# Attention with image prompts on one core: the last batch's turns, scores and query chunk in other places, and the root of the batch before it behind the last exponentials

## The chip, the core and the metric

The kernel runs on one NeuronCore of a Trainium2 chip. The metric is the time of one execution on the device, in microseconds (us). The core's engines each work through their own instructions in order and wait for one another through semaphores: PE (TensorE, matmuls; PEld is its weight load), DVE (VectorE), ACT (ScalarE), POOL (GpSimdE), and SP (SyncE), which here issues nearly all DMA transfers.

## The reference

`x` has 8 batches of 112 queries by 320 channels, the context 8 batches of 375 rows by 512 (371 of text, 4 of image prompts); there are 20 heads of 16 channels.

```python
def _l2norm(x, axis=-1):
    n = jnp.sqrt(jnp.sum(x * x, axis=axis, keepdims=True))
    return x / jnp.maximum(n, EPS)
...
text_ehs = encoder_hidden_states[:, :-NUM_TOKENS]
ip_ehs = encoder_hidden_states[:, -NUM_TOKENS:]
...
q = heads(hidden_states @ W_q)
k_t = heads(text_ehs @ W_k)
v_t = heads(text_ehs @ W_v)
scores_t = jnp.einsum('bhsd,bhtd->bhst', q, k_t) * attn_scale
probs_t = jax.nn.softmax(scores_t, axis=-1)
text_out = jnp.einsum('bhst,bhtd->bhsd', probs_t, v_t)
...
k_ip = heads(ip_ehs @ W_k_ip)
v_ip = heads(ip_ehs @ W_v_ip)
attn_scores = jnp.einsum('bhsd,bhnd->bhsn', q, k_ip) * attn_scale
qsem = jnp.einsum('bhst,bte->bhse', probs_t, text_ehs)
qsem = _l2norm(qsem)
ip_n = _l2norm(ip_ehs)
sem = jnp.einsum('bhse,bne->bhsn', qsem, ip_n)
...
fused = attn_scores + SEM_SCALE * sem
probs_ip = jax.nn.softmax(fused, axis=-1)
probs_ip = probs_ip * spatial_mask[None, None, :, None]
ip_out = jnp.einsum('bhsn,bhnd->bhsd', probs_ip, v_ip)
...
out = text_out + IP_SCALE * ip_out
out = out @ W_out + b_out
out = out + residual
```

## The kernel before

Batches are numbered 0 to 7; "the sixth batch" is number 6, "the last" number 7. The 20 heads of a batch form five groups of four. All numbers are 32-bit floats.

**A group's way.** `scores` multiplies a head's queries (`qm`, scaled and masked by `project_queries`) by its keys `kT` into one PSUM bank. `maxima` reduces it on DVE (`nmx`), `exponentials` takes the exponential on ACT into `p` and copies four prompt columns into `ipl`. `sent` has SP move the exponentials into one of two buffers `xg`, laid out in 32-row blocks, and `turned` transposes such a buffer on DVE into `xgT`, in pieces; a piece is one `next`. `multiplied` is the main work of PE: twelve steps `j`, in each of which four heads multiply `xgT` by a piece of `u`, with 392 columns at the first step and 32 fewer at each further one. `u` holds the context's Gram matrix (`gram`), since the norm in the reference is a quadratic form of the probabilities, and behind it the values, which `placed` copies for the next group on POOL in three copies, one per four steps. Each of them overwrites what four steps of the group before read, and each is waited for by the four steps that read it.

**The sums behind a group.** The quadratic form of a head is the row sum of a product of the bank and `p`. `reduced` does both on DVE in one pass (`junk`). To spare DVE, `shared` does some heads otherwise, in three pieces: copies on ACT into `shared` (and of the 21 columns that hold the prompts' products, the sum of exponentials and the values into `pvs`), products on POOL, row sums on ACT into `ss`. The last group of batch 6 has two heads done so, groups 0 to 3 of batch 7 have 3, 3, 2 and 1.

**A batch's end.** `finish` is cut into pieces too: `z2` and the reciprocal `zr` on DVE and `attn` on POOL; `rn` on DVE, its root on ACT, with ACT's table of functions loaded for the root ahead of it and for the exponential behind it; the logits `fu` on DVE; their exponential `ex`; the weights `w`; and then matmuls, which for batch 6 come after all groups of batch 7.

**Order.** It is written by hand: each engine takes its instructions in the order in which the code emits them. The main loop goes over batches 0 to 6 and within each group emits the scores and the turns of groups to come; batch 7 has a loop of its own at the end, which the change rewrites. There group g's banks come from `ps_qd` (four banks) for even g and from the two small pools of two banks for odd g. The scores of group 3 use the small pools' banks, which group 1 takes next; those of group 4 use `ps_qd`'s, which group 0 had and group 2 takes next. The last chunk of channels of batch 7's queries (`ps_q_7_2`, heads of group 4) are projected between groups 0 and 1.

## Time and profile before

| | |
|---|---|
| median of 3 runs (lowest to highest) | 410.84 us (410.69 to 410.94) |
| the profiled execution: its time, and its span from first to last instruction | 410.67 us, 409.0 us |
| mean granted clock of PE | 0.989 |
| ACT, DVE, POOL, share of the span busy | 47%, 83%, 29% |
| transfers, share of 16 DMA engines | about 52%; next to none in the last 20 us |
| last batch's loop, first matmul of group 0 to the first step behind group 4 | 364.88 to 397.16 us of the span |
| last write of the output issued | 405.98 us of the span |

The page gives each engine's busy time and cuts the span into 40 slices with a digit for the busy tenths, and a line PEclk for the share of PE's clock that was granted. The chain of waits is read backward from the last instruction: at each step what released it. The order of time lists an engine's instructions with their start, length and, in brackets, how long the engine stood idle ahead of them and who ended that. Windows give the busy time of each engine in a stretch.

### The profile page before, as it was taken

How to read it: one execution, taken by the hardware profiler on the slowest of the kernel's cores; microseconds unless marked ns; L12 is line 12 of the kernel's file. 1: busy time of each engine (PE TensorE's matmuls, PEld its weight loads, DVE VectorE, ACT ScalarE, POOL GpSimd, SP SyncE). 2: the span in 40 equal slices, each digit the busy share in tenths (PEclk: the TensorE clock that was granted, in tenths of full speed). 3: DMA queues.
4: the chain of work that ended last, by engine and by line, in shares of the span. 5: the costliest groups of instructions: out<-in, count | busy, mean ns of one | idle time of the engine just before them, and what ended most of it. 6: DMA issues, size and time to landing. Idle time of an engine off the chain costs nothing.

```text
span 409.0 us, 13891 instructions
## 1 busy us (share of the span) xinstructions
PE 400.4 (98%) x5442; PEld 314.2 (77%) x5442; DVE 340.3 (83%) x731; ACT 191.7 (47%) x663; POOL 118.3 (29%) x282
## 2 busy tenths in 40 slices
PE   9999999999999999999999999999999999996996
PEld 8658777987788877787778877788777977785893
DVE  4678787888998898788998989788998888877774
ACT  3554243454344633446344543456334463567663
POOL 6611110111432206122162214222060211735340
PEclk9999999999999999999999999999999999997999
DMA  6984665556555556366555555465444455444200
GB/s 215 216 184 112 218 170 150 143 159 175 144 138 136 153 137 153 105 169 168 133 143 126 151 138 139 120 148 158 128 119 120 122 172 142 119 119 125 67 3 30
DMA packets 46433, 56.94 MB, mean 139 GB/s; under 512 B 9405, under 2 KB 40961, under 8 KB 46368
## 3 DMA queue, kind: packets, MB, share of 16 engines
q1 hardware_dynamic: 46328, 55.99, 51.9%
q8 instruction: 43, 0.70, 0.7%
q14 instruction: 22, 0.18, 0.1%
q10 hardware_dynamic: 40, 0.07, 0.0%
HBM read 15.88 MB, written 1.39 MB: 42 GB/s over the span
## 4 chain that ended last, share of the span: by engine, by line
PE 96%; ACT 1%; issue 1%; POOL 1%; DVE 1%; POOLq 0%; DVEq 0%
PE ps_qd L729 41%; PE ps_k L547 15%; PE ps_s L658 11%; PE ps_v L547 10%; PE ps_g L513 7%; PE ps_q L363 4%; PE ps_o L949 3%; PE ps_g L469 1%; PE ps_w L448 1%; PE ps_o L900 1%; POOL shared L764 0%; PE ps_a L937 0%; DVE xgT L710 0%; PE ps_c L432 0%; PE ps_ipkv L298 0%
## 5 line engine op out<-in xcount | busy, mean ns | idle before, releaser
L729 PE MATMUL ps_qd<-u,xgT 32*112 32x168 f32 (+11 forms) x3840 | 218.2, 352 | 0.0
L729 PEld LDWEIGHTS ps_qd<-u,xgT 32*112 32x112 f32 x3840 | 185.5, 173 | 26.3 <-issue 2.3
L694 ACT ACTIVATE p<-ps_s,nmx 112x371 f32<-112x371 f32 x156 | 84.5, 579 | 97.3 <-DVE nmx L680 92.3
L710 DVE STREAM_TRANSPOSE xgT<-xg 128x512 f32<-128x512 f32 (+2 forms) x79 | 125.9, 1602 | 1.1 <-DMA xr_sb<-in_x_dram 0.5
L680 DVE TENSOR_REDUCE nmx<-ps_s 112x1 f32<-112x371 f32 x160 | 78.7, 536 | 28.1 <-PE ps_s L658 23.6
L775 DVE CUSTOM_DVE_ANT_0 junk<-ps_qd,p 112x371 f32<-112x371 f32 x146 | 79.3, 543 | 20.1 <-ACT pvs L742 4.0
L627 POOL COPY u<-vr 128x64 f32<-128x64 f32 x120 | 26.5, 240 | 145.4 <-PE ps_qd L729 100.3
L658 PE MATMUL ps_s<-kT,qm 32*112 32x375 f32 (+1 forms) x320 | 65.4, 497 | 0.0
L547 PE MATMUL ps_k<-ctxT,wk_sb 128*128 128x371 f32 x192 | 64.6, 484 | 0.0
L547 PEld LDWEIGHTS ps_k<-ctxT,wk_sb 128*128 128x128 f32 x192 | 35.1, 190 | 20.3 <-ACT vT L569 0.5
L547 PE MATMUL ps_v<-ctxT,wv_sb 128*128 128x371 f32 x128 | 42.4, 482 | 0.0
L658 PEld LDWEIGHTS ps_s<-kT,qm 32*112 32x112 f32 x320 | 25.6, 173 | 12.8 <-issue 11.0
L547 PEld LDWEIGHTS ps_v<-ctxT,wv_sb 128*128 128x128 f32 x128 | 23.7, 190 | 14.5 <-issue 0.5
L513 PE MATMUL ps_g<-ctxT 128*32 128x375 f32 (+11 forms) x672 | 30.4, 333 | 0.0
L513 PEld LDWEIGHTS ps_g<-ctxT 128*32 128x32 f32 x672 | 27.7, 110 | 2.0
L562 ACT COPY kT<-ps_k 128x371 f32<-128x371 f32 x24 | 11.2, 468 | 37.8 <-PE ps_k L547 37.8
L696 ACT COPY ipl<-ps_s 112x4 f32<-112x4 f32 x140 | 23.1, 165 | 0.0
L420 DVE STREAM_TRANSPOSE ctxT<-ct 128x512 f32<-128x512 f32 x21 | 22.7, 1093 | 0.0
L924 POOL TENSOR_TENSOR wv<-vip,w 112x1280 f32<-112x1280 f32 x6 | 14.8, 2465 | 26.5 <-DVE w L858 26.5
L363 PE MATMUL ps_q<-xT,wq_sb 128*128 128x224 f32 (+1 forms) x90 | 17.5, 335 | 3.5 <-ACT shared L760 3.5
L485 ACT ACTIVATE ug<-ps_g 128x375 f32<-128x375 f32 (+2 forms) x24 | 8.3, 375 | 24.4 <-issue 9.0
L569 ACT COPY vT<-ps_v 128x371 f32<-128x371 f32 x16 | 7.5, 468 | 25.4 <-PE ps_v L547 25.4
(164 smaller groups left out, 313.2 us busy)
## 6 DMA issues: line engine op xcount, KB each, us to landing
xg<-p SPq DMA_DIRECT2D x156, 162.3 KB
u<-ug SPq DMA_DIRECT2D x122, 99.0 KB
ct<-in_ctx_dram SPq DMA_DIRECT2D x28, 176.0 KB
vip<-vipd SPq DMA_DIRECT2D x6, 560.0 KB
xr_sb<-in_x_dram SPq DMA_DIRECT2D x32, 35.0 KB
out_dram<-ob SPq DMA_DIRECT2D x8, 140.0 KB
x_sb<-in_x_dram SPq DMA_DIRECT2D x6, 140.0 KB
xg<-wv_sb SPq DMA_DIRECT2D x4, 162.3 KB
```

The lines of the kernel that those rows point to most:

```text
L363: nc.tensor.matmul(ps[:, : n * S], wq_sb[:, j, i * P : (i + 1) * P], xT[:, j, :n, :, : S // QN], start=(j == 0), stop=(j == NC - 1),)
L420: nc.vector.transpose(ctxT[:, :, c * P : (c + 1) * P].rearrange("p e (j i) -> p j e i", i=RG), ct[:, some, :].rearrange("p j (k e) -> p j ...
L513: nc.tensor.matmul(ps[c][q * RG : (q + 1) * RG, j * RG - c * P : T - c * P], ctxT[:, e, j * RG : (j + 1) * RG], ctxT[:, e, j * RG : T], st ...
L547: nc.tensor.matmul(ps[:, :TT], w[:, e, i * P : (i + 1) * P], ctxT[:, e, :TT], start=(e == 0), stop=(e == NE - 1),)
L627: nc.gpsimd.tensor_copy(v, dealt(b, c, s["vr"][:, c * QN : (c + 1) * QN, min(g + g // NE, 2 * NC - 1), :]))
L658: nc.tensor.matmul(ps[:S, :w], qm[a * RG : (a + 1) * RG, i, r, j * S : (j + 1) * S], s["kT"][a * RG : (a + 1) * RG, i, :w], start=True, st ...
L680: nc.vector.tensor_reduce(nmx, s["sc", g, a][:S, :TT], AX.X, ALU.max, negate=True)
L694: nc.scalar.activation(s["p", g][:, a, :], ps[:S, :TT], AF.Exp, bias=nmx)
L696: nc.scalar.copy(s["ipl"][:, groups[g][a], :], ps[:S, TT:T])
L710: nc.vector.transpose(xT[:, j0:j1].rearrange("p j (k q) -> p q j k", q=QN), xg[:, :, j0 * RG : j1 * RG].rearrange("p q (j k) -> p q j k", ...
L729: nc.tensor.matmul(banks[a][:S, j * RG : UW], xT[a * RG : (a + 1) * RG, j, :S], region(b, c)[a * RG : (a + 1) * RG, q, j * RG - c * P :], ...
L775: nc.vector.tensor_tensor_reduce(out=junk, in0=ps[:S, :TT], in1=s["p", g][:, a, :], scale=1.0, scalar=0.0, op0=ALU.mult, op1=ALU.add, accu ...
```

## The change

Only the last batch's loop is rewritten, and two special cases in `project_queries` go. The queries' last chunk is projected ahead of group 0, into the common banks, and scaled on ACT. `finish` of batch 6 begins behind group 0 instead of ahead of it; the second and third pieces of the row sums shared with ACT are emitted later; its root, with both table loads, stands behind the last exponentials. `turned` is taken in halves, with maxima between them. The scores of group 4 move from steps 2 and 3 of group 1 to steps 5 and 6. The later pieces of `finish` come one or two places later.

```diff
--- before.py
+++ after.py
@@ -339,7 +339,6 @@
 
     def project_queries(bs):
         n = len(bs)
-        end = bs[0] == B - 1
         xT = work.tile([P, NC, 2, QN, RG], F32, tag="xT", name=f"xT_{bs[0]}", bufs=1)
         qm = work.tile([P, NC, 2, 2 * S], F32, tag="qm", name=f"qm_{bs[0]}", bufs=2)
 
@@ -355,10 +354,7 @@
                 )
             yield
         for i in range(NC):
-            if end and i == FULL:
-                ps = ps_qd.tile([P, 512], F32, tag="qd", name=f"ps_q_{bs[0]}_{i}")
-            else:
-                ps = bank(f"ps_q_{bs[0]}_{i}", spare=(bs[0], i) == (1, 1))
+            ps = bank(f"ps_q_{bs[0]}_{i}", spare=(bs[0], i) == (1, 1))
             for j in range(NC):
                 nc.tensor.matmul(
                     ps[:, : n * S],
@@ -369,9 +365,7 @@
                 )
 
             for r in range(2 if i < FULL else 1):
-                by = nc.vector.tensor_scalar_mul
-                if qT is None and not (end and i == FULL):
-                    by = nc.scalar.mul
+                by = nc.scalar.mul if qT is None else nc.vector.tensor_scalar_mul
                 by(qm[:, i, r, : n * S], ps[:, : n * S], emask[:, r : r + 1])
             if qT is not None:
                 nc.scalar.copy(qT[:, i, :], ps[:, :S])
@@ -1291,42 +1285,38 @@
             drain(prompt_logits(b))
 
 
-    next(sums)
     b = B - 1
     before = ("f", b - 1)
-
-    run(before, lambda: finish(b - 1, bd=bd[:, 0]))
-    with_bias(b - 1)
-    nc.scalar.preload_act_table(AF.Sqrt)
+    next(sums)
+    run(("q", b), None)
 
     for g in range(NG):
-        if g == 1:
-            run(("q", b), None)
-            drain(sums)
         for j, _ in enumerate(multiplied(b, g)):
-            if g == 0 and j == 0:
-                drain(sums)
             if g == 0 and j in (0, 3):
-                for a in (2, 3) if j == 0 else (0, 1):
+                some = (2, 3) if j == 0 else (0, 1)
+                for a in some:
                     scores(b, NG - 2, a, ps=bank(f"ps_s_{b}_{NG - 2}_{a}", spare=a > 1))
+                for a in some:
+                    probabilities(b, NG - 2, a, hold=True)
                 if j == 0:
-                    for a in (2, 3):
-                        maxima(b, NG - 2, a)
-                    run(before, None)
-                    for a in (2, 3):
-                        exponentials(b, NG - 2, a)
-                    drain(turned(b, 1))
-                    for a in (2, 3):
+                    turn = turned(b, 1)
+                    next(turn)
+                else:
+                    drain(turn, sums)
+                    for a in (2, 3, 0, 1):
                         sent(b, NG - 2, a)
-                else:
-                    for a in (0, 1):
-                        probabilities(b, NG - 2, a)
-            if g == 1 and j in (2, 3):
-                for a in ((3, 2), (1, 0))[j - 2]:
+            if g == 1 and j in (5, 6):
+                for a in ((3, 2), (1, 0))[j - 5]:
                     ps = ps_qd.tile([P, 512], F32, tag="qd", name=f"ps_s_{b}_{NG - 1}_{a}")
                     scores(b, NG - 1, a, ps=ps)
-                    probabilities(b, NG - 1, a)
-            if (g, j) in ((1, QN), (1, 2 * QN), (2, 2 * QN)):
+                    probabilities(b, NG - 1, a, hold=True)
+                if j == 6:
+                    drain(turn)
+                    for a in (3, 2, 1, 0):
+                        sent(b, NG - 1, a)
+                    nc.scalar.preload_act_table(AF.Sqrt)
+                    run(before, None)
+            if (g, j) in ((2, QN), (2, 2 * QN), (3, QN)):
                 run(before, None)
             if g > 1 and j == 2 * QN:
                 drain(sums)
@@ -1335,15 +1325,21 @@
         if g == NG - 1:
             break
         n = (3, 3, 2, 1)[g]
-        sums = shared(b, g, n)
+        earlier, sums = sums, shared(b, g, n)
         next(sums)
         reduced(b, g, n)
         if g < NG - 2:
             value_sums(b, g, n)
-            drain(turned(b, g + 2))
+            turn = turned(b, g + 2)
+            if g == 0:
+                next(turn)
+            else:
+                drain(turn, earlier)
             placed(b, g + 1, range(NT) if g == 0 else (NT - 1,))
             next(sums)
         if g == 0:
+            run(before, lambda: finish(b - 1, bd=bd[:, 0]))
+            with_bias(b - 1)
             with_bias(b)
             run(("f", b - 2), None)
         if g == 2:
```

The lines of the changed program are four to six less than those of before, so `L710` and `L704` are one line of code.

**DVE, from the sums of batch 6's last group on.** Names: `junk` and `ss` are `reduced`, `z`, `zr`, `rn` are `finish` of batch 6, `nmx_3_2` is the maximum for group 3's head 2, `xgT_1` the turned group 1. Before:

```order
L825 SCALAR_TENSOR_TENSOR z_6_0_5235<-pvs_3352 112x20
L816 RECIPROCAL zr_0_5237<-pvs_3352 112x20
L680 TENSOR_REDUCE nmx_3_2_5258<-ps_s_3_2_5254 112x1
L680 TENSOR_REDUCE nmx_3_3_5260<-ps_s_3_3_5256 112x1
L830 TENSOR_TENSOR rn_0_5236<-ss_3351,z_6_0_5235 112x20
L710 STREAM_TRANSPOSE xgT_1_5269<-xg_151 128x4x192 x2
L680 TENSOR_REDUCE nmx_3_0_5290<-ps_s_3_0_5286 112x1
L680 TENSOR_REDUCE nmx_3_1_5295<-ps_s_3_1_5288 112x1
L775 ISA junk_6_5339,ss_4038<-ps_qd_0_3_5247,p_0_4977 112x371
L775 ISA ss_4038 112x1
L710 STREAM_TRANSPOSE xgT_2_5342<-xg_152 128x4x192 x2
L375 TENSOR_SCALAR qm_4305<-ps_q_2_5353,emask 128x112
```

and with the change:

```order
L674 TENSOR_REDUCE nmx_3_2_5252<-ps_s_3_2_5248 112x1
L674 TENSOR_REDUCE nmx_3_3_5256<-ps_s_3_3_5250 112x1
L704 STREAM_TRANSPOSE xgT_1_5260<-xg_151 128x4x192
L674 TENSOR_REDUCE nmx_3_0_5278<-ps_s_3_0_5274 112x1
L674 TENSOR_REDUCE nmx_3_1_5282<-ps_s_3_1_5276 112x1
L704 STREAM_TRANSPOSE xgT_1_5260<-xg_151 128x4x192
L769 ISA junk_6_5332,ss_4038<-ps_qd_0_3_5243,p_0_4977 112x371
L769 ISA ss_4038 112x1
L704 STREAM_TRANSPOSE xgT_2_5335<-xg_152 128x4x192
L819 SCALAR_TENSOR_TENSOR z_6_0_5343<-pvs_3352 112x20
L810 RECIPROCAL zr_0_5345<-pvs_3352 112x20
L674 TENSOR_REDUCE nmx_4_3_5384<-ps_s_4_3_5382 112x1
```

`z`, `zr` and `rn` no longer stand ahead of group 1's turn (`rn`, which waits for ACT's sums, comes five rows further on than the rows shown), the maxima of group 3's heads 0 and 1 stand between its halves, and the last maxima between the halves of group 2's turn.

**POOL, from batch 6's products on.** Names: `ob` and `xb` are outputs and residuals, `shared` the products, `attn` the divided values, `u<-vr` is `placed`. Before:

```order
L913 TENSOR_TENSOR ob_5230<-ob_5230,xb_4703 112x320
L764 TENSOR_TENSOR shared_4_5215<-shared_4_5215,p_4_4839 112x371 x2
L817 TENSOR_TENSOR attn_153<-pvs_3352,zr_0_5237 112x320
L789 TENSOR_TENSOR xb_5238<-x_sb,bias_sb 112x320
L627 COPY u_4035<-vr_4036 128x4x16 x3
L764 TENSOR_TENSOR shared_0_5332<-shared_0_5332,p_0_4977 112x371 x3
L789 TENSOR_TENSOR bd<-x_sb,bias_sb 112x320
L627 COPY u_4035<-vr_4036 128x4x16 x3
L764 TENSOR_TENSOR shared_1_5453<-shared_1_5453,p_1_5038 112x371 x3
```

and with the change:

```order
L907 TENSOR_TENSOR ob_5230<-ob_5230,xb_4703 112x320
L758 TENSOR_TENSOR shared_4_5215<-shared_4_5215,p_4_4839 112x371 x2
L621 COPY u_4035<-vr_4036 128x4x16 x3
L758 TENSOR_TENSOR shared_0_5325<-shared_0_5325,p_0_4977 112x371 x3
L811 TENSOR_TENSOR attn_153<-pvs_3352,zr_0_5345 112x320
L783 TENSOR_TENSOR xb_5346<-x_sb,bias_sb 112x320
L783 TENSOR_TENSOR bd<-x_sb,bias_sb 112x320
L621 COPY u_4035<-vr_4036 128x4x16 x3
L758 TENSOR_TENSOR shared_1_5441<-shared_1_5441,p_1_5038 112x371 x3
```

`attn` and `xb` moved from ahead of group 1's placing to behind the three products of group 0, and the placing of group 2's values still stands behind them.

**ACT, from group 0's row sums on.** Names: `p_4` are group 4's exponentials, `ex` and `rn` belong to `finish` of batch 6, `shared_1` is group 1's copy. Before:

```order
L768 ACTIVATE shared_0_5332,ss_4038<-shared_0_5332 112x371 x3
L694 ACTIVATE p_4_5381<-ps_s_4_3_5377,nmx_4_3_5379 112x371
L696 COPY ipl_4037<-ps_s_4_3_5377 112x4
L694 ACTIVATE p_4_5381<-ps_s_4_2_5385,nmx_4_2_5387 112x371
L696 COPY ipl_4037<-ps_s_4_2_5385 112x4
L694 ACTIVATE p_4_5381<-ps_s_4_1_5396,nmx_4_1_5398 112x371
L696 COPY ipl_4037<-ps_s_4_1_5396 112x4
L694 ACTIVATE p_4_5381<-ps_s_4_0_5403,nmx_4_0_5405 112x371
L696 COPY ipl_4037<-ps_s_4_0_5403 112x4
L850 ACTIVATE ex_0_5439<-fu_0_5416 112x80
L759 COPY pvs_4039<-ps_qd_1_0_5361 112x21
L760 COPY shared_1_5453<-ps_qd_1_0_5361 112x371
```

and with the change:

```order
L688 ACTIVATE p_4_5386<-ps_s_4_3_5382,nmx_4_3_5384 112x371
L690 COPY ipl_4037<-ps_s_4_3_5382 112x4
L688 ACTIVATE p_4_5386<-ps_s_4_2_5389,nmx_4_2_5391 112x371
L690 COPY ipl_4037<-ps_s_4_2_5389 112x4
L688 ACTIVATE p_4_5386<-ps_s_4_1_5399,nmx_4_1_5401 112x371
L690 COPY ipl_4037<-ps_s_4_1_5399 112x4
L688 ACTIVATE p_4_5386<-ps_s_4_0_5405,nmx_4_0_5407 112x371
L690 COPY ipl_4037<-ps_s_4_0_5405 112x4
L1317 ACT_TABLE_LOAD
L828 ACTIVATE rn_0_5344<-rn_0_5344 112x20
L829 ACT_TABLE_LOAD
L753 COPY pvs_4039<-ps_qd_1_0_5353 112x21
```

The sums of group 0 moved behind the copies of group 1, and between the last exponentials and those copies stand two table loads with the root between them. Before, the two loads and the root stood ahead of the exponentials of group 3.

## The prediction

> **What bounds the kernel now.** I read the page first (engines, slices), then the chain of waits over the last 90 us, then windows of the stretch that stands out, then each engine's order of time there.
>
> ```profile
> span 409.0 us, 13891 instructions
> PE 400.4 (98%) x5442; PEld 314.2 (77%) x5442; DVE 340.3 (83%) x731; ACT 191.7 (47%) x663; POOL 118.3 (29%) x282
> PE   9999999999999999999999999999999999996996
> PEclk9999999999999999999999999999999999997999
> ```
>
> PE sets the time: busy 98%, every slice full but one near the end, and in that slice the granted clock is low too. The chain of waits shows what happens there.
>
> ```profile
> 356.50 0.67 PE ps_q L363 x6
> ...
> 368.88 0.03 DVE rn L830
> ...
> 370.68 1.17 issue
> 371.84 0.49 DVE nmx L680
> ...
> 373.59 0.38 ACT shared L760
> ...
> 374.01 1.63 PE ps_q L363 x6
> 375.63 4.37 PE ps_qd L729 x26
> ```
>
> Group 0 of the last batch is finished, and PE waits. What it waits for runs from `rn` (the root's operand of the sixth batch) through both half-turns and the maxima on DVE, then exponentials and copies on ACT, to the queries' last chunk. The windows price it (columns: length, PE, PEld, DVE, ACT, POOL busy, granted clock, DMA share, GB/s).
>
> ```profile
> 364.96:370.51 5.55, 5.55 (x104) 5.14 (x104) 3.00 (x9) 4.32 (x8) 3.42 (x4) 1.00 0.63 174
> 370.51:374.01 3.50, 0.00 (x1) 0.00 (x1) 3.50 (x7) 2.90 (x13) 1.39 (x4) 0.86 0.11 24
> 374.01:375.63 1.62, 1.62 (x10) 1.42 (x10) 1.62 (x2) 1.50 (x7) 1.60 (x2) 0.50 0.63 184
> 375.63:380.00 4.37, 4.37 (x33) 2.56 (x36) 0.60 (x2) 1.24 (x5) 1.93 (x3) 0.51 0.32 97
> 392.51:397.16 4.65, 4.65 (x99) 4.60 (x93) 3.34 (x14) 3.21 (x10) 2.07 (x4) 1.00 0.01 4
> 372.00:373.00 1.00, 0.00 (x0) 0.00 (x0) 1.00 (x3) 0.64 (x3) 0.27 (x2) 1.00 0.00 0
> 373.00:374.00 1.00, 0.00 (x0) 0.00 (x0) 1.00 (x3) 1.00 (x6) 0.00 (x0) 0.52 0.38 83
> 379.00:380.00 1.00, 1.00 (x12) 0.61 (x12) 0.00 (x0) 0.00 (x0) 0.00 (x0) 0.56 0.00 0
> 380.00:381.00 1.00, 1.00 (x22) 0.90 (x20) 0.58 (x2) 0.00 (x0) 0.00 (x0) 1.00 0.00 0
> ```
>
> PE stands still for 3.50 us, and the clock falls to half at about 373.0, some 2.5 us after PE stopped, until about 379.9. The place thus costs three things: 3.50 of idling; 1.63 - 0.67 = 0.96 for the six `ps_q` instructions at half clock (the same six took 0.67 at 356.50); and half of the 4.25 us from 375.63 to 379.88, 2.12, for group 1. Sum **6.58**: what there is to win. Without it the five groups would end at 397.16 - 6.58 = 390.6. A group with four scores takes 5.55 (first row), one without 4.65 (fifth row).
>
> **The change part by part.** Where "after" times stand below, they are sums from the rows, on before's time axis; up to 363 the order is the same.
>
> *Queries' last chunk ahead of group 0.* The six instructions now follow L949 at full clock: 0.67, so group 0 ends at 371.18 instead of 370.51. Its bank is free, as its earlier user's exponentials lie far back. Its scaling moves from DVE to ACT, ahead of the exponentials, into the place of a table load. That is no extra term: the 0.67 is already in the 6.58.
>
> *Root off DVE's and ACT's front, turns in halves.*
>
> ```profile
> 366.47 1.00 DVE L680 TENSOR_REDUCE nmx<-ps_s 112x1 f32<-112x371 f32 x2 [1.13 <-PE ps_s L658]
> 368.88 0.18 DVE L830 TENSOR_TENSOR rn<-ss,z 112x20 f32<-112x20 f32 x1 [1.42 <-ACT shared L768]
> 369.06 2.93 DVE L710 STREAM_TRANSPOSE xgT<-xg 128x768 f32<-128x768 f32 x2
> 371.84 0.94 DVE L680 TENSOR_REDUCE nmx<-ps_s 112x1 f32<-112x371 f32 x2
> 372.36 0.57 ACT L694 ACTIVATE wv_sb<-ps_s,nmx 112x371 f32<-112x371 f32 x1 [0.58 <-DVE nmx L680]
> 372.87 0.58 ACT L694 ACTIVATE wv_sb<-ps_s,nmx 112x371 f32<-112x371 f32 x1
> 373.44 0.51 ACT L760 COPY shared<-ps_qd 112x371 f32<-112x371 f32 x1
> 373.87 0.53 ACT L760 COPY shared<-ps_qd 112x371 f32<-112x371 f32 x1
> ```
>
> DVE stood 1.42 us for the sixth batch's sums. Now: two maxima from 366.47 + 0.67 = 367.14, first half-turn 368.0 to 369.5 (2.93 for two), the other maxima to 370.4, second half-turn to 371.9. The exponentials follow at a pitch of 0.51 and are done, with their small copies, at 371.15. Group 1 takes the four banks of these scores; its first matmuls need the first half-turn (369.5) and the exponentials, its seventh step the second half-turn, over 3 us later. So it starts at about 371.2, with 0 to 0.2 us of waiting; I take **0.1**. The old gap is gone. The transposes' sources have landed: the row of 372 to 373 has a DMA share of 0.00, and the next are sent at 371.9 (SP's order is unchanged, first send 372.06 before).
>
> *What the moved work meets: POOL.*
>
> ```profile
> 366.32 1.90 POOL L764 TENSOR_TENSOR shared<-shared,p 112x371 f32<-112x371 f32 x2
> 368.18 0.74 POOL L817 TENSOR_TENSOR attn<-pvs,zr 112x320 f32<-112x320 f32 x1
> 370.88 0.86 POOL L789 TENSOR_TENSOR xb<-x_sb,bias_sb 112x320 f32<-112x320 f32 x1 [1.96 <-DMA x_sb<-in_x_dram]
> 374.03 2.71 POOL L764 TENSOR_TENSOR shared<-shared,p 112x371 f32<-112x371 f32 x3 [1.76 <-ACT shared L760]
> 376.70 0.86 POOL L789 TENSOR_TENSOR bd<-x_sb,bias_sb 112x320 f32<-112x320 f32 x1
> 387.23 0.42 POOL L627 COPY u<-vr 128x64 f32<-128x64 f32 x2
> 390.77 0.51 ACT L768 ACTIVATE shared<-shared 112x371 f32<-112x371 f32 x1
> 391.29 0.50 ACT L768 ACTIVATE shared<-shared 112x371 f32<-112x371 f32 x1
> ```
>
> `placed`, the three copies of the next group's values into `u`, stands behind this in POOL's order, and a group's first matmul waits for the first copy. In POOL's idle stretch before 374 lay `attn` (0.74) and `xb` (0.86); now both stand behind group 0's products. ACT does two sums first (371.05 to 372.1, pitch 0.52 as at 390.77 and 391.29), then the first `shared` copy to 372.65. POOL: three products 372.7 to 375.4 (2.71), `attn` to 376.15, `xb` to 377.0, `bd` to 377.85, first copy (half of 0.42) to 378.05. Group 1 ends at 371.2 + 5.55 = 376.75. So PE waits **1.3** for group 2, where before it waited for nothing. PE restarts from standstill, so the overlap between neighbouring groups is lost as well: between 0 and one matmul (352 ns in the next fence); I take 0.2, so **1.5**.
>
> ```profile
> L729 PE MATMUL ps_qd<-u,xgT 32*112 32x168 f32 (+11 forms) x3840 | 218.2, 352 | 0.0
> 369.33 1.28 ACT L835 ACT_TABLE_LOAD   x1
> 372.06 3.52 SPq L701 DMA_DIRECT2D xg<-wv_sb  x4
> 378.00:379.00 1.00, 1.00 (x12) 0.57 (x8) 0.00 (x0) 0.00 (x0) 0.00 (x0) 0.50 0.00 0
> ```
>
> *Last scores later, the root behind them: ACT.* Before, the scores stood after steps 2 and 3 of group 1; now after steps 5 and 6. The first six of a group's twelve steps hold 72% of its columns (392 down to 232 of 392 down to 40), 3.35 of 4.65 us: the scores come near 374.5 and 375.2. The four maxima (0.47 each) end at 376.9, the exponentials at 377.65: just before the 378.05 from POOL, so group 2's banks are no longer wait. Behind the exponentials come a table load (1.28), the root (0.2; `rn` on DVE is ready at 378.4, after a half-turn) and another load (1.28): to 380.4. Only then does ACT copy group 1 for POOL: three copies at a pitch of 0.43. POOL multiplies from 381.05 to 383.75 and places group 3's first values at 383.95. Group 2, started at 378.05, ends at 382.7. A second wait: 1.25, with the restart **1.4**. The two loads, 2.56, are not new (before they lay ahead of the exponentials of group 3's weights), but here POOL and then PE stand behind them.
>
> *Behind that.* ACT is through with six sums and the sixth batch's exponential at 385.7, copies group 2 to 386.7, POOL's two products end at 388.2 and the next placing at 388.4, just under group 3's end of 388.65: no wait, with 0.2 to spare. DVE turns group 3 from 379.0, after its source (sent 371.9 to 375.4; at 378 to 379 the DMA share is 0.00 even in before), and group 4 from 384.5, its source sent 378.4 to 382.0. The closing chain after group 4 keeps its order and moves as a whole.
>
> **Sum:** 6.58 - 0.1 - 1.5 - 1.4 = 3.58, taken as 3.5. The profiled execution took 410.67 (span 409.0 and 1.67 around it); 407.2 against it, and the median of the runs lies 0.17 above: **407.3**. The unseen prices: each POOL wait between 0 (POOL that much sooner, as in before) and 2.5, where the clock's fall begins to be seen; the small wait at group 1 between 0 and 0.7 (both half-turns needed).
>
> **Rule and row on the clock.** The Trainium skill's page "TensorE: Matmul & The Clock Gate", Part 1, lets the clock fall after a whole idle window of about 3.4 us. Here it fell 2.5 us after the last matmul, so a window with some work in it was enough; by the page's rule the two new gaps leave the clock alone. The same page's section "A second HAM failure mode: psum-queue depth-cycling" speaks against the change: short idles between matmul groups made the clock swing there. No trace here shows it for gaps of 1.5 us.
>
> **Rivals.**
> - *The clock falls in a new gap.* For: it fell after 2.5 us, and two gaps come within 6 us. Against: each is 1.5 at most in my sum, and the one gap of before was 3.50. Price: some 6.9 us at half (373.0 to 379.9), 3.4 lost. After the first gap it hides the second wait, since group 2 then lasts past 384: 407.3 + 3.4 - 1.4 = 409.3; after the second: 410.7. Chance 0.12.
> - *No new wait.* POOL gets to `placed` in time. For: 29% busy over the span. Against: its order above. 410.84 - 6.5 = 404.3. Chance 0.08.
> - *The halves don't free group 1* (the change doesn't do what it says): it starts after the second half-turn, at 371.9; 408.0. Chance 0.05.
> - *Slower: the copies of group 1 come so late on ACT that group 3's gap reaches 2.5 us and the clock falls there.* It decides from a first copy at 381.6 instead of 380.4, for which every step ahead (four exponentials, two loads, the root) would have to slip by 0.17. Price: 1.2 more waiting and 3.4 of clock: 407.3 + 4.6 = 411.9. Against: each step has its own row. Chance 0.04.
>
> **How the numbers follow.** The forecast has 0.71, with 405.8 to 408.6 as its own range. No new wait (0.08) reaches below, the clock above; 404.9 to 409.4 leaves out the bottom of the one, the late half of the other and the slower case. A measurement here can tell 0.2% (0.8 us, 410.0) from no change: faster 0.91 (forecast, no wait, halves, the clock after the first gap), same 0.05, slower 0.04.
>
> **What would show it.** Right: no idle near 371 and `ps_q` at about 0.67 with the clock at 1.00; PE gaps of 1 to 2 us ahead of groups 2 and 3, ended by POOL's copy into `u`; group 4 ending near 393.6. Wrong: a PEclk below 1.00 between 372 and 392; a gap ended by ACT or DVE; no gap at all; or a longer closing chain after group 4.

## The result and the profile after

| | before | after |
|---|---|---|
| median of 4 runs each, side by side (lowest to highest) | 410.76 us (410.46 to 410.94) | 407.47 us (407.25 to 407.81) |
| ratio, 95% interval | | 0.9921 [0.9904, 0.9938] |
| the profiled execution: time, span | 410.67 us, 409.0 us | 407.31 us, 405.6 us |
| mean granted clock of PE | 0.989 | 0.999 |

The kernel became 3.3 us faster; 407.3 had been forecast, with a range of 404.9 to 409.4. The page of the changed kernel, its engines and slices:

```profile
span 405.6 us, 13896 instructions
PE 398.2 (98%) x5442; PEld 313.9 (77%) x5442; DVE 341.1 (84%) x730; ACT 190.6 (47%) x664; POOL 118.2 (29%) x282
PE   9999999999999999999999999999999999999796
PEclk9999999999999999999999999999999999999999
```

PEclk has lost its 7, and of PE's slices one near the end shows a 7 where one of before showed a 6. The chain of waits in the last batch (start, length, what) says what lies there now:

```profile
365.03 0.66 PE ps_q L359 x6
...
372.72 1.37 POOL shared L758 x2
...
375.49 0.51 POOL attn L811
...
376.16 0.65 POOL xb L783
```

The queries' last chunk takes 0.66 us, the full-clock price, and the chain then runs through POOL: the products of group 0, `attn`, `xb`. In order of time, with the idle time ahead of each row in brackets, PE's two stops and POOL's work ahead of them:

```profile
378.06 5.11 PE L723 MATMUL ps_qd<-u,xgT 32*112 32x392 f32 x96 [1.38 <-POOL u L621]
384.58 9.61 PE L723 MATMUL ps_qd<-u,xgT 32*112 32x392 f32 x192 [1.41 <-POOL u L621]
```
```profile
372.72 2.78 POOL L758 TENSOR_TENSOR shared<-shared,p 112x371 f32<-112x371 f32 x3 [1.19 <-ACT shared L754]
375.46 0.74 POOL L811 TENSOR_TENSOR attn<-pvs,zr 112x320 f32<-112x320 f32 x1
376.16 0.86 POOL L783 TENSOR_TENSOR xb<-x_sb,bias_sb 112x320 f32<-112x320 f32 x1
376.97 0.86 POOL L783 TENSOR_TENSOR bd<-x_sb,bias_sb 112x320 f32<-112x320 f32 x1
377.78 0.58 POOL L621 COPY u<-vr 128x64 f32<-128x64 f32 x3
381.58 2.75 POOL L758 TENSOR_TENSOR shared<-shared,p 112x371 f32<-112x371 f32 x3 [3.22 <-ACT shared L754]
```

The first stop ends with the first of the three copies that begin at 377.78, the second with the one behind the products of 381.58. The bracket on that last row leads on to ACT, whose order of time around the root reads:

```profile
377.44 0.62 ACT L688 ACTIVATE p<-ps_s,nmx 112x371 f32<-112x371 f32 x1
377.90 0.21 ACT L690 COPY ipl<-ps_s 112x4 f32<-112x4 f32 x1
378.13 1.28 ACT L1317 ACT_TABLE_LOAD   x1
379.42 0.22 ACT L828 ACTIVATE rn<-rn 112x20 f32<-112x20 f32 x1
379.66 1.28 ACT L829 ACT_TABLE_LOAD   x1
380.95 0.18 ACT L753 COPY pvs<-ps_qd 112x21 f32<-112x21 f32 x1
```

The last exponential ends at 378.06; load, root and load fill ACT to 380.94; only then are group 1's banks copied for POOL. So the change exchanges one stop of 3.50 us, which also halved the clock, for two of 1.4 us, which did not. The experiments ask whether each stop has the cause named, why the clock held, and which parts of the change earned the gain.

### The profile page after: what moved, and what is told of

The parts are those of the page before. It is cut to its first block, busy times and chain, and to the rows that moved or that the text cites. A ratio compares the mean times of both kernels' runs of the same rounds, so it can differ in the third digit from the quotient of the medians.

```text
span 405.6 us, 13896 instructions
## 1 busy us (share of the span) xinstructions
PE 398.2 (98%) x5442; PEld 313.9 (77%) x5442; DVE 341.1 (84%) x730; ACT 190.6 (47%) x664; POOL 118.2 (29%) x282
## 3 DMA queue, kind: packets, MB, share of 16 engines
HBM read 15.88 MB, written 1.39 MB: 43 GB/s over the span
## 4 chain that ended last, share of the span: by engine, by line
PE 95%; POOL 1%; issue 1%; ACT 1%; DVE 1%; POOLq 0%; DVEq 0%
PE ps_qd L723 40%; PE ps_k L541 16%; PE ps_s L652 11%; PE ps_v L541 10%; PE ps_g L507 7%; PE ps_q L359 4%; PE ps_o L943 3%; PE ps_g L463 1%; POOL shared L758 1%; PE ps_w L442 1%; PE ps_o L894 1%; PE ps_c L426 0%; PE ps_a L931 0%; PE ps_ipkv L298 0%; DVE nmx L674 0%
## 5 line engine op out<-in xcount | busy, mean ns | idle before, releaser
L704 DVE STREAM_TRANSPOSE xgT<-xg 128x512 f32<-128x512 f32 (+2 forms) x79 | 126.0, 1598 | 0.7 <-DMA xr_sb<-in_x_dram 0.4
L480 POOL TENSOR_TENSOR ug<-ug,half 128x128 f32<-128x128 f32 (+1 forms) x24 | 10.4, 447 | 28.1 <-ACT ug L479 28.1
```

The lines of the kernel that those rows point to most:

```text
L704: nc.vector.transpose(xT[:, j0:j1].rearrange("p j (k q) -> p q j k", q=QN), xg[:, :, j0 * RG : j1 * RG].rearrange("p q (j k) -> p q j k", ...
```

## The experiments

Edits are against the changed kernel unless the text says otherwise. All of these kernels compute the reference in full. "First" and "second" gap are the stops of PE ahead of groups 2 and 3.

| kernel | median (lowest to highest), runs | ratio to before, interval |
|---|---|---|
| changed kernel again | 407.59 (407.22 to 408.04), 6 | 0.9923 [0.9905, 0.994] |
| before, with the query chunk moved alone | 408.41 (407.31 to 408.89), 6 | 0.9932 [0.9912, 0.9952] |
| POOL's `attn`, `xb`, `bd` behind the first copy | 408.03 (407.25 to 409.8), 7 | 0.9942 [0.9921, 0.9963] |
| `bd` computed three times | 409.98 (409.08 to 411.07), 10 | 0.9976 [0.996, 0.9992] |
| root behind ACT's copies of group 1 | 407.02 (406.27 to 407.39), 6 | 0.9905 [0.9887, 0.9922] |
| last scores back at steps 2 and 3 | 406.58 (406.21 to 406.94), 6 | 0.9895 [0.9874, 0.9916] |
| root back at the front | 409.66 (408.15 to 410.35), 12 | 0.9961 [0.9944, 0.9977] |
| two shared heads in group 1 | 409.2 (407.38 to 410.22), 10 | 0.995 [0.9932, 0.9968] |
| first turn whole again | 410.15 (408.41 to 411.05), 12 | 0.9976 [0.9958, 0.9994] |
| rearranged | 406.54 (405.9 to 406.87), 6 | 0.9895 [0.9878, 0.9913] |
| rearranged, less work on DVE | 407.96 (405.69 to 409.61), 7 | 0.992 [0.9891, 0.995] |

**The changed kernel again**, beside three of the experiments.

> The changed kernel itself, on the chip and in the hour of the three others. Theory: gaps of about 1.4 us ahead of groups 2 and 3, wherever the clock's windows of 3.41 us lie, leave the clock at 1.00, since a window with 1.42 us of standstill kept it in the run with more work on POOL, while one with 1.59 lost it in the run with the placing first: so all its times lie together, 407.2 to 408. Rival (the 1.4 us gaps drop the clock in some executions): a second cluster near 409.5.

Gaps of 1.39 and 1.41 us, full clock. With the first four runs that makes ten executions, none above 408.04 and with mean clocks of 0.997 to 1.000. A stretch of 3.41 us at half clock would lower the mean to 0.996, so the clock did not fall while PE had work; in the two profiled executions it falls only behind the last matmul.

**The query chunk alone.** The kernel before, with the six `ps_q` instructions ahead of group 0 (and the scaling on ACT), and nothing else.

```diff
+    run(("q", b), None)
 ...
     run(before, lambda: finish(b - 1, bd=bd[:, 0]))
 ...
         if g == 1:
-            run(("q", b), None)
             drain(sums)
```

> The kernel before with one part of the change: the queries' last chunk goes ahead of group 0, into the common banks, scaled on ACT. The root, the turns and the last scores stay. In before, the chunk waited for a copy of group 0 (374.0), while the exponentials that group 1 waits for ended at about 373.5. Theory A (the chunk's bank wait ended the gap, the exponentials behind the half-turns come next): PE stands still from 371.2 to 373.5, 2.3 us. If the clock holds through 2.3 us, no later gap follows, because POOL and ACT keep their order of before: 410.8 - 1.2 (gap) - 1.0 (chunk at full clock) - 2.1 (group 1 at full clock) = 406.5, better than the whole change. Theory B (the clock falls in a gap of 2.3 us too): group 1 at half clock again, 408.6. Rival C (the root's wait holds everything, the chunk was hidden behind it): 410 to 411.

PE's order of time:

```profile
374.10 4.07 PE L723 MATMUL ps_qd<-u,xgT 32*112 32x392 f32 x27 [2.14 <-POOL u L621]
```

The one gap shrinks from 3.50 to 2.14 us. The copies into `u` that the bracket names were done by 373.10; it is the banks that come late, so group 1 waits for the exponentials behind the root (those of heads 0 and 1 begin at 373.37 and 373.88), as Theory A had it. The chunk's own clock loss is gone. But the clock fell here too, for one stretch of 3.41 us (375.46 to 378.87) instead of the 6.83 of before's profiled run, which Theory A had not expected; so the time lies between the two theories. In the one run of 407.31 the clock held (mean 0.998; the other five 0.993 to 0.996). This edit alone brings 2.4 of the 3.3 us.

**The first gap: POOL's order.** `attn`, `xb` and `bd` are emitted behind the first copy of group 2's values, that is, at step 3 of group 1.

```diff
         if g == 0:
-            run(before, lambda: finish(b - 1, bd=bd[:, 0]))
-            with_bias(b - 1)
-            with_bias(b)
 ...
                 placed(b, g + 1, (j // QN,))
+            if g == 1 and j == QN - 1:
+                run(before, lambda: finish(b - 1, bd=bd[:, 0]))
+                with_bias(b - 1)
+                with_bias(b)
```

> The changed kernel, with the sixth batch's attn and xb and the last batch's bd on POOL moved behind the first copy of group 2's values. Theory: the gap ahead of group 2 shrinks from 1.38 us to below 1, since the last exponentials hold its banks until 378.1, but group 3 still starts at 384.6, because that start hangs on ACT's late copies of group 1; the gap ahead of group 3 grows by what the other lost. Time 407.4, no change. Rival (each gap costs by itself): 406.0 to 406.4.

PE's order of time has no stop ahead of group 2 any more. The next one is this:

```profile
385.38 10.85 PE L723 MATMUL ps_qd<-u,xgT 32*112 32x392 f32 x174 [1.59 <-POOL u L621]
```

So the first gap was POOL's, and taking it away gains nothing: counted from the first matmul of group 0 (366.46 here, 365.62 in the changed kernel), group 3 begins at 18.92 against 18.96. It waits for ACT's row, which does not move. The two gaps overlap in what they cost, which the prediction's sum, one term for each, does not say. The times fall into two sorts: four runs from 407.25 to 408.03, and three from 409.67 to 409.8 with a mean clock of 0.993. The profiled execution is of the second sort, and its windows (length, PE, PEld, DVE, ACT, POOL busy, granted clock, DMA share, GB/s) show a gap of only 1.59 us halving the clock:

```profile
385.00:386.00 1.00, 0.62 (x5) 0.63 (x9) 0.86 (x4) 0.68 (x4) 0.67 (x4) 0.83 0.00 0
386.00:387.00 1.00, 1.00 (x10) 1.00 (x8) 1.00 (x3) 1.00 (x6) 0.00 (x0) 0.50 0.08 16
389.00:390.00 1.00, 1.00 (x23) 1.00 (x20) 0.85 (x4) 0.99 (x4) 0.49 (x1) 0.96 0.00 0
```

Half clock from about 385.7 to 389.1: ten matmuls in a microsecond instead of 23.

**The first gap lengthened.** `bd` is computed three times in a row, the same values each time.

```diff
             with_bias(b)
+            with_bias(b)
+            with_bias(b)
```

> The changed kernel, with the last batch's residual plus bias computed three times instead of once on POOL (twice 0.86 us more, the same values), ahead of group 2's placing. The gap ahead of group 2 grows from 1.38 to 3.1 us. Theory A (slack, and the clock holds): group 2 ends at 384.9, after the placing of group 3 at 384.5, so the second gap vanishes and the time stays at 407.4 to 407.8. Theory B (the clock falls in a gap of 3.1 us, as it did in before): up to 3.4 us more, 409 to 411. Rival C (both gaps stay): 409.1.

```profile
380.77 15.46 PE L723 MATMUL ps_qd<-u,xgT 32*112 32x392 f32 x270 [3.28 <-POOL u L621]
```

Two sums of 0.86 us more on POOL made the gap 1.9 us longer, 3.28, and the second gap went (PE's row runs on over it): the first gap is set by POOL's row, to the last `bd`. The clock fell in all ten runs (means 0.989 to 0.996), in the profiled one for 3.41 us (382.32 to 385.74), as Theory B had it.

**The second gap: the root on ACT.** The two loads and the root are emitted behind ACT's copies of group 1.

```diff
                     for a in (3, 2, 1, 0):
                         sent(b, NG - 1, a)
-                    nc.scalar.preload_act_table(AF.Sqrt)
-                    run(before, None)
 ...
             value_sums(b, g, n)
+            if g == 1:
+                nc.scalar.preload_act_table(AF.Sqrt)
+                run(before, None)
```

> The changed kernel with the root and its two table loads behind ACT's copies of group 1 instead of ahead of them. Theory (the 2.8 us of loads and root make the copies, POOL's products and so group 3 late): the gap of 1.41 us ahead of group 3 vanishes, the one ahead of group 2 stays; the loads then delay the copies of group 2, so a gap of about 1.1 us appears ahead of group 4; net 0.1 to 0.8 us faster than the changed kernel in the same session. Rival (POOL alone makes group 3 late): the gap stays at 1.4.

PE's order of time:

```profile
378.88 9.70 PE L723 MATMUL ps_qd<-u,xgT 32*112 32x392 f32 x192 [1.37 <-POOL u L621]
389.09 4.90 PE L723 MATMUL ps_qd<-u,xgT 32*112 32x392 f32 x96 [0.51 <-POOL u L621]
```

The second gap is gone, the first stays at 1.37, and a small one of 0.51 (1.1 had been expected) opens ahead of group 4, where the work that was pushed back is late in its turn. The net is 0.6 us against the changed kernel run beside it.

**The same row, begun sooner.** The scores of group 4 return to steps 2 and 3 of group 1; the rest stays as changed.

```diff
-            if g == 1 and j in (5, 6):
-                for a in ((3, 2), (1, 0))[j - 5]:
+            if g == 1 and j in (2, 3):
+                for a in ((3, 2), (1, 0))[j - 2]:
 ...
-                if j == 6:
+                if j == 3:
```

> The changed kernel with the scores of group 4 back at steps 2 and 3 of group 1; all else as changed. Theory A (what holds group 3 is ACT's row: last exponentials, two table loads, root, then the copies of group 1): the row begins about 1.5 us earlier, so the gap ahead of group 3 falls from 1.4 to 0.3 us or less; the gap ahead of group 2, which POOL sets, stays at 1.3 to 1.5 us; PE may wait up to 0.4 us inside group 1 for the banks of group 0, which the copies and sums free. About 406.5, 0.8 to 1.3 less than the changed kernel run beside. Theory B (the exponentials wait for DVE's sums of group 0 in any place, so ACT's row does not begin sooner): the gap ahead of group 3 stays within 0.3 us of 1.4, and the time is that of the changed kernel or later by the waits inside group 1, 407.5 to 408.5.

ACT's and then PE's order of time:

```profile
377.05 1.28 ACT L1317 ACT_TABLE_LOAD   x1
379.88 0.18 ACT L753 COPY pvs<-ps_qd 112x21 f32<-112x21 f32 x1
```
```profile
378.33 14.93 PE L723 MATMUL ps_qd<-u,xgT 32*112 32x392 f32 x288 [1.32 <-POOL u L621]
```

Counted from group 0's first matmul (365.89 here, 365.62 in the changed kernel), ACT's row is 1.3 us sooner; the second gap is gone, and groups 2 to 4 run through in 14.93 us. That is Theory A in every point. The median is 406.58; the changed kernel, which was not run beside it, had 407.47 and 407.59: the later place of the last scores, one of the parts of the change, costs about 1 us by itself.

**The root back at the front.** `finish` begins ahead of group 0, and the sums, both loads and the root stand ahead of all exponentials of group 3, as before the change; chunk, halves and later scores are kept.

```diff
+    run(before, lambda: finish(b - 1, bd=bd[:, 0]))
+    with_bias(b - 1)
+    nc.scalar.preload_act_table(AF.Sqrt)
 ...
                 for a in some:
-                    probabilities(b, NG - 2, a, hold=True)
+                    maxima(b, NG - 2, a)
+                if j == 0:
+                    drain(sums)
+                    run(before, None)
+                for a in some:
+                    exponentials(b, NG - 2, a)
 ...
-                    nc.scalar.preload_act_table(AF.Sqrt)
-                    run(before, None)
 ...
-            run(before, lambda: finish(b - 1, bd=bd[:, 0]))
-            with_bias(b - 1)
```

> The changed kernel with the sixth batch's root, its two table loads, its sums, attn and xb back at the front of the last batch (ahead of the exponentials of group 3's heads 2 and 3), as before the change; the query chunk, the halves and the later last scores are kept. Theory A (the changed kernel's two gaps come from where the root and finish stand: POOL's attn and xb for the first, the root and its loads on ACT for the second): both gaps of 1.4 us ahead of groups 2 and 3 go, to under 0.5 us each, and in their place PE waits ahead of group 1, about 1.0 to 2.0 us, since group 3's exponentials stand behind the root again. Net gain over the changed kernel 0.5 to 1.5 us where that one gap stays under 1.4 us and the clock holds (about 406.5), and no gain, about 408, where the gap is over 1.45 us and one window of 3.41 us runs at half clock. Theory B (the gaps come from the shared copies and the halves themselves, the place of the root does not matter): the gaps ahead of groups 2 and 3 stay at 1.2 us or more, and a third is added ahead of group 1: 409 or later.

```profile
372.84 5.74 PE L723 MATMUL ps_qd<-u,xgT 32*112 32x392 f32 x51 [1.44 <-POOL u L621]
```

The gaps are as Theory A said: 1.44 ahead of group 1, none ahead of groups 2 and 3. The time is not: 409.4 to 410.35 in the seven runs with a mean clock of 0.995 or 0.996, and 408.15 to 408.81 in the five where it held, so with a full clock too it is later than the changed kernel, where some 406.5 had been expected. In the profiled run, ACT's last exponentials follow at a pitch of 0.51 us and end at 381.81, and the first matmuls of group 2's heads begin about 0.5 us apart (380.39, 380.87, 381.39, 381.92), each some 0.1 us after an exponential, as the banks come free: waits too short to show as idle, which were not tried apart. So with the other parts as they are, the root's move is worth about 0.9 us at full clock (the median of those five runs is 408.5), and 2 with the clock.

**Less for ACT and POOL ahead of group 3.** Two instead of three heads of group 1 are shared; DVE does the third.

```diff
-        n = (3, 3, 2, 1)[g]
+        n = (3, 2, 2, 1)[g]
```

> The changed kernel, with two heads of group 1 instead of three summed by way of ACT and POOL; DVE takes the third. POOL's products before group 3's placing are two instead of three (0.92 us less). Theory: the gap ahead of group 3 falls from 1.41 to about 0.5 us, the one ahead of group 2 stays, time 406.5. Rival (DVE's extra 0.7 us makes the turn of group 3 late): 407.4 or above.

```profile
378.85 5.11 PE L723 MATMUL ps_qd<-u,xgT 32*112 32x392 f32 x96 [1.42 <-POOL u L621]
384.48 9.77 PE L723 MATMUL ps_qd<-u,xgT 32*112 32x392 f32 x192 [0.52 <-POOL u L621]
```

The gaps are as expected: the second falls by 0.9, what one product takes, and the first stays. The time is 1.6 us worse than the changed kernel's instead of better: in the closing chain PE stops for 0.85 us (397.63 to 398.49) until POOL's `attn`, behind DVE's last row sums, and the clock falls for 3.41 us behind it. These sums begin 1.48 us after group 4's end, 0.99 in the changed kernel; that the pass which DVE took on makes them late is likely, but not shown, and one of them then waits another 0.5 us, as it does in before and in the rearranged kernel below, for a cause that was not tried. Most of the loss is the clock: the four runs with a mean clock of 0.997 or 0.999 took 407.38 to 408.62, with a median about 0.3 us above the changed kernel's.

**The halves undone.** Group 1's turn is taken in one go, ahead of the maxima of heads 0 and 1.

```diff
                     turn = turned(b, 1)
-                    next(turn)
+                    drain(turn)
```

> The changed kernel with the turn of group 1 whole again ahead of the second pair of maxima. Theory: maxima, exponentials and the copies behind them come one half-turn (1.45 us) later, group 1 starts 1.4 us after group 0's end instead of at once, and everything behind shifts: 1.4 us slower than the changed kernel in the same session, or 3.1 where the clock falls. Rival (the gaps ahead of groups 2 and 3 take it up): no slower than 0.3 us.

DVE's and PE's order of time:

```profile
368.79 2.99 DVE L704 STREAM_TRANSPOSE xgT<-xg 128x768 f32<-128x768 f32 x2
371.64 0.93 DVE L674 TENSOR_REDUCE nmx<-ps_s 112x1 f32<-112x371 f32 x2
```
```profile
372.87 4.05 PE L723 MATMUL ps_qd<-u,xgT 32*112 32x392 f32 x51 [1.15 <-POOL u L621]
380.09 5.11 PE L723 MATMUL ps_qd<-u,xgT 32*112 32x392 f32 x96 [1.31 <-POOL u L621]
386.64 9.69 PE L723 MATMUL ps_qd<-u,xgT 32*112 32x392 f32 x140 [1.44 <-POOL u L621]
```

The maxima come after the whole turn, and a gap of 1.15 us opens ahead of group 1; the other two stay. (The releaser named is the copy into `u`; the first of those copies was long done, so it is the banks, that is, the exponentials behind these maxima.) The third gap is 1.44, and the clock falls behind it in the profiled run and, by the means of 0.994 to 0.996, in five of twelve (410.31 to 411.05). Beside the chunk and the root's place the halves are worth 2.6 us on the median, and 1.7 against the seven runs whose clock held (median 409.29).

**Rearranged.** Root and loads in ACT's idle time behind its copies of group 0; the sums of batch 6 at step 2 of group 0; `finish` begun ahead of group 0, so that `attn` stands where POOL is idle; `xb` and `bd` behind the first copy; the last scores after steps 4 and 5.

```diff
     run(("q", b), None)
+    run(before, lambda: finish(b - 1, bd=bd[:, 0]))
 ...
+            if g == 0 and j == 2:
+                drain(sums)
 ...
-            if g == 1 and j in (5, 6):
+            if g == 1 and j in (4, 5):
 ...
-                    nc.scalar.preload_act_table(AF.Sqrt)
-                    run(before, None)
 ...
+            if g == 1 and j == QN - 1:
+                with_bias(b - 1)
+                with_bias(b)
 ...
             value_sums(b, g, n)
+            if g == 0:
+                nc.scalar.preload_act_table(AF.Sqrt)
+                run(before, None)
 ...
-            run(before, lambda: finish(b - 1, bd=bd[:, 0]))
-            with_bias(b - 1)
-            with_bias(b)
```

> A rearrangement of the changed kernel. ACT's two sums of the sixth batch stand between the two pairs of exponentials of group 3, the root with its loads in ACT's idle time between the copies of group 0 and the last exponentials, the reciprocals and attn at the front, xb and bd behind the first copy of group 2's values, the last scores one step earlier. Theory: both gaps vanish, group 3 starts about 2.2 us earlier than in the changed kernel; DVE, then without idle time, holds the end back: 1.2 to 1.8 us faster than the changed kernel in the same session. Rival (ACT's exponentials now end later and a gap of more than 1.5 us stays ahead of group 2, or the clock falls): same or slower.

```profile
388.04 4.90 PE L723 MATMUL ps_qd<-u,xgT 32*112 32x392 f32 x96 [0.19 <-POOL u L621]
397.11 0.31 PE L1006 MATMUL ps_a<-ident,attn 112*128 112x112 f32 x1 [0.84 <-POOL attn L997]
```

Both gaps are gone, the clock stays at 1.00, and with 406.54 this kernel is 4.2 us under the before run beside it, level with the 406.58 above and 1.0 under the changed kernel, a little less than the 1.2 to 1.8 expected. What is left is a stop of 0.84 in the closing chain, behind DVE's row sums.

**Rearranged, with DVE relieved.** The edit is against the rearranged kernel: one head more of group 2 is shared, and the exponential and weights of batch 6 come ahead of group 4's turn.

```diff
-        n = (3, 3, 2, 1)[g]
+        n = (3, 3, 3, 1)[g]
 ...
-            if (g, j) in ((2, QN), (2, 2 * QN), (3, QN)):
+            if (g, j) == (2, QN):
                 run(before, None)
 ...
+            if g == 2:
+                run(before, None, 2)
```

> The rearranged kernel root_in_idle with three instead of two heads of group 2 shared with ACT and POOL, and the exponential and the weights of the sixth batch's prompts ahead of group 4's turn. Theory A (in root_in_idle DVE holds the end: its chain of logits and weights delays the last rows): DVE loses a pass of about 0.8 us over one bank ahead of the closing chain, the gap of 0.84 us there shrinks to under 0.3 us, and the time falls by 0.3 to 0.7 us to about 406.0. Theory B (POOL or ACT, with one more head, is late for group 4's values instead): a gap ahead of group 4 of 0.6 us or more, and no gain, 406.5 to 407.2.

```profile
394.20 0.47 PE L878 MATMUL ps_a<-wT,bd 80*128 80x112 f32 x2 [0.85 <-ACT wT L864]
```

No gap ahead of group 4, so Theory B fails; DVE's stop is gone too. But 0.85 us of stop has come in a new place, at the head of the closing chain, where ACT copies `wT` only behind a table load and an exponential. In this execution some 0.48 of it come from further up that row: DVE's `rn` took 0.65 us instead of 0.17, beside POOL's `attn` (see the last section). Whether the runs without that delay are the two fastest is not on record. In two runs the clock held: 405.69 and 405.78, 0.8 us under the kernel it is made from. In the other five it fell, by the means of 0.996 and 0.989 once or twice, and they take 407.21 to 409.61. On the median that is a loss.

## Why the prediction was right

- *What there is to win, 6.58.* All of it came: PE's row has no stop near 371, `ps_q` takes 0.66 us, PEclk is full. The wait of 0.1 at group 1 was about right, and undoing the halves brings back a gap of 1.15 there, which shows that they are what frees group 1.
- *First gap, 1.3 forecast, 1.38 measured, from POOL's order.* Shown twice: the gap goes when `attn`, `xb` and `bd` stand behind the copy, and grows by what is added to that row.
- *Second gap, 1.25 forecast, 1.41 measured, from ACT's row with the root.* Shown twice as well: it goes when the root stands behind the copies, and when the row begins 1.3 us sooner.
- *No wait at group 4.* Right: the row of 384.58 runs through both groups.
- *The terms that were mis-sized.* Group 4 ended at 394.12, not 393.6. Half a microsecond was lost on ACT's row (first copy at 380.95, not 380.4, as the last exponential ended at 378.06, not 377.65), while the second gap grew by less, since group 2 itself ended late: alone between two stops it took 5.11 us, not the 4.65 of a group that follows another without a stop. So the loss at a restart is nearer 0.4 than the 0.2 taken. Against that stands the closing chain, which did not move "as a whole": from `ps_wT` to the end of the last matmul it took 7.92 us (394.12 to 402.04), before 8.26 (397.16 to 405.42). In the trace of before one of DVE's last row sums stood idle for 0.49 us, in the changed kernel's none did. That cannot be put down to the change: the chain took 7.92 us with the query chunk alone too (395.72 to 403.64), and 8.40 in the repeat of the changed kernel (394.32 to 402.72), so it varies between executions of one kernel by more than the 0.34 in question. That the two errors all but cancel, 3.36 us between the two profiled executions against 3.5 forecast, is luck.

The rows of the two last matmuls, before and after:

```profile
404.63 0.79 PE L1047 MATMUL ps_o<-bw,wT_last 16*112 16x320 f32 x2
```
```profile
401.25 0.79 PE L1041 MATMUL ps_o<-bw,wT_last 16*112 16x320 f32 x2
```

- *The clock.* It held, in all ten executions, as forecast, but with far less to spare than the text had it. The bound for each wait, "2.5, where the clock's fall begins to be seen", was wrong: gaps of 1.44 and 1.59 us halved it in other kernels, and the changed kernel's are 1.38 to 1.41. The rival of a fall in a new gap was given 0.12; it lay a few hundredths of a microsecond away.
- *What the sum hid.* Two gaps that are each real need not each be worth their length: without the first, the second starts at the same time and grows. And of the parts, the later scores cost 1 us that the forecast's reckoning never priced as an alternative.

## What to carry to other kernels

Find out for a stop of the main engine not only who ends it but who would end the next one: here removing the first gap alone gained nothing, and shortening ACT's row gained 0.6 to 1 us. Price a table load by what stands behind it in the engine's order, and put it where that engine waits for others anyway. Treat a gap near the length that costs the clock as worth 1.7 us more than it shows, and look at several executions, since the same gap may cost it in one and not in the next.

## What the runs showed of the hardware

**The clock falls after much shorter stops than expected.** In the profiled runs the clock fell behind stops of 1.44 (root at the front; the third of the whole turns), 1.59, 2.14 and 3.28 us, and held behind 1.15, 1.31, 1.32 and 1.37 to 1.42. Each fall lasted 3.41 us, or 6.83 in before's profiled run, which looks like a grid of windows of 3.41 us that is not tied to the stops. The stretches at full clock fit it: with the chunk alone the clock is full from 378.87 to 406.18, eight times 3.41. Counted on that grid, between groups the clock fell where a single window held 1.44 us or more of a stop, and stayed up where it held 1.42 or less. With `bd` computed three times, the window up to 378.91 held 1.42 us of the stop that began at 377.49 and left the clock up; the next held 1.86 and cost it. A window already at half clock stayed there with less: in before the one after the fall held almost 1 us of the stop. In the changed kernel's two profiled executions the grid cut each stop in two, with at most 0.96 us in one window. The grid would also explain why the clock held in some runs of one kernel and not in others (one of six with the chunk alone, five of twelve with the root at the front). Before varies as well: of its 61 runs beside the experiments, 26 have a mean clock of 0.994 or 0.996, as for one window lost, and a median of 410.4, and 35 have 0.989 to 0.992, as for two, and 411.24. So the 6.58 of the prediction belong to the dearer kind of execution. The Trainium skill's page "TensorE: Matmul & The Clock Gate", Part 1, has a free-running window of about 3.4 us too, but lets the clock fall after a whole idle one. These runs do not agree: less than half of a window without work was enough. In the closing chain, where short instructions stand, a stop of 0.85 cost the clock in two kernels and one of 0.84 did not in a third; what counts there was not settled.

**Two executions differ by 0.85 us from the start.** Two windows of the changed kernel's profiled run and of the last experiment's, at the same place of the program (columns as above):

```profile
5.00:6.00 1.00, 1.00 (x9) 1.00 (x10) 0.66 (x3) 0.24 (x2) 0.48 (x9) 1.00 0.92 318
6.00:7.00 1.00, 1.00 (x11) 1.00 (x11) 0.97 (x3) 0.65 (x3) 0.00 (x0) 1.00 0.67 173
```
```profile
5.00:6.00 1.00, 1.00 (x5) 1.00 (x6) 0.62 (x2) 0.30 (x2) 0.48 (x9) 1.00 0.86 292
6.00:7.00 1.00, 1.00 (x7) 1.00 (x6) 0.95 (x3) 0.00 (x0) 0.00 (x0) 1.00 0.72 196
```

The clock column says 1.00 in all four, but PE gets through 9 and 11 matmuls in the one and through 5 and 7 in the other, so it comes up to speed later. Its `ps_q` of the last batch then begin at 364.87 and 365.72. The two programs are the same up to there, so the edits have no part in it. It does not account for the two clusters in the changed kernel's repeat, 407.22 to 407.3 and 407.87 to 408.04: its two profiled executions, of 407.31 and 407.97, begin `ps_q` at 364.87 and 365.05, only 0.18 apart. The rows at the end of the next part show the rest.

**DVE's work on two tensors slows beside POOL's products.** DVE's order of time in the changed kernel, with POOL's products running from 381.58 to 384.33:

```profile
382.13 0.52 DVE L836 TENSOR_TENSOR fu<-pvs,rn 112x80 f32<-112x80 f32 x1
382.69 0.94 DVE L837 SCALAR_TENSOR_TENSOR fu<-fu,ipl 112x80 f32<-112x80 f32 x1
383.67 0.24 DVE L839 TENSOR_REDUCE mx<-fu 112x20 f32<-112x80 f32 x1
```

With the root behind the copies, `L836` and `L837` came at 383.47 and 383.75, when POOL's products were done (at 382.18), and took 0.24 each; a short copy of POOL's beside `L836` left no mark on it. The reduction, which reads one tensor, took 0.24 both times. The Trainium skill's page "SBUF — State Buffer", section "SBUF: two separate sides", says that the two engines lock a pair of ports from each other for a whole instruction; the rows of the products agree.

The same meeting separates the changed kernel's two profiled executions. When the first 16 heads of batch 7 are finished, DVE's `rn` and POOL's `attn` for them become ready at the same moment. First the execution of 407.31, then the one of 407.97:

```profile
392.22 0.17 DVE L824 TENSOR_TENSOR rn<-ss,z 112x16 f32<-112x16 f32 x1
392.22 0.67 POOL L811 TENSOR_TENSOR attn<-pvs,zr 112x256 f32<-112x256 f32 x1 [1.02 <-ACT shared L762]
```
```profile
392.42 0.65 DVE L824 TENSOR_TENSOR rn<-ss,z 112x16 f32<-112x16 f32 x1 [0.15 <-ACT shared L762]
392.41 0.63 POOL L811 TENSOR_TENSOR attn<-pvs,zr 112x256 f32<-112x256 f32 x1 [1.01 <-ACT shared L762]
```

Where `rn` lost, it took 0.48 us more, the root and the logits behind it came later by as much, PE's stop ahead of the last `attn` grew from 0.17 to 0.49, and the closing chain from 7.92 to 8.40. Of the 13 profiled executions in this document two show the long `rn`, this one and that of the last experiment; no run was made to keep the two instructions apart.
